# Weighed rows of the first sixteen expert blocks parked in DRAM until the edges are done

## The chip, the cores and the metric

The kernel runs on one core of one Trainium2 chip. Its time is the device time of one execution in microseconds (us). The profile is of one execution, with each instruction's start and duration on the engines: PE (TensorE; PEld is its weight loading), DVE (VectorE), ACT (ScalarE), POOL (GpSimd) and SP (SyncE, which here only issues DMAs).

## What is computed

A graph attention layer with a feed-forward net is followed by a mixture of experts. There are 6,250 nodes of 256 features, 100,000 edges sorted by their target, and 8 experts of which each token takes two. Cut to what matters:

```python
xn = layer_norm(x); h = (xn @ W).reshape(N, 8, 32)
e = leaky_relu(a_src[src] + a_dst[dst])
alpha = softmax of e over the edges of one dst
out = segment_sum(h[src] * alpha, dst) + xn @ W_res + bias
out = layer_norm(out)
x = x + out + gelu_tanh(out @ w1 + b1) @ w2 + b2

probs = softmax(norm(x) @ Wr + br);  top_p, top_idx = top_k(probs, 2)
y_e = gelu(ln_e(norm(x)) @ W1[e] + b1[e]) @ W2[e] + b2[e]      # W1[e]: 256 x 1024
x = x + sum over the two chosen e of weight_e * y_e
```

## The kernel before

**Stages.** First the node tables are written to DRAM (to about 115 us). Then the edges run, from the last target node down, in steps of four tiles of 128 edges: a step gathers the source rows (`fetch`, four indirect DMAs on POOL, L873), weighs them on DVE (`weigh`, L917 to L921) and adds them by target node on PE (`add_tiles`, L936). There are `NG` = 196 such steps, each spread over six steps of the program (`LASTST` = 6): the gather of a step is issued three steps ahead of its product on DVE, into four buffers, and the second to fourth gather of a step also wait for ACT's work of the step ahead. When the nodes of a unit (256 rows) have all their edges, the node net runs for them, their rows are stored to `out` and routed: each row goes, with its token's number and weights, into a list of rows for each expert in DRAM (`scatter`, indirect DMAs on POOL, L1470).

**Blocks.** As soon as an expert has 256 rows, a block of them can run, while edges are still going on. There are `NS` = 53 blocks, three of them half blocks. A block loads its expert's weights (1 MB each for the two products, L1525 and L1533) and its rows (L1541) by SP, runs the two products on PE (`up`, L1054, and `down`, L1067), adds the bias on DVE (`finish`, L1573, into `yb`, three buffers), multiplies by the token's weight on ACT (`weigh_block`, L856 through the helper `act`), and adds the result to the tokens' rows in `out` (`give_back`, L1583): for each 128 rows one indirect DMA on POOL that accumulates in DRAM. Since two blocks can hold the same token, the first accumulating DMA of a block waits until those of the block before have landed; the two of one block don't wait for each other.

**The planner.** The order of all work on each engine is fixed when the program is built. `task` names a piece of work with its engine, a cost and the tasks that must lie a number of steps before it; `run_tasks` goes through the list of waiting tasks at each step, oldest first, and issues what is due as long as its engine has room. The room of a step is 7.5 for PE and 2.6 for POOL while edges run (less what the edges take), and 3.9 and 2.6 behind them. A give-back costs 2.6, so a step takes one of them, or one scatter. SP's tasks cost nothing. Steps from `NG + LASTST` = 202 on have no edges; there the edges' buffers are given up and a third set of weight buffers is opened (L1662 to L1664). SP and POOL carry out their instructions in the program's order: one that waits holds up all behind it on that engine.

Of the kernel before, what the change touches and what calls it, by code (L numbers as in the profile page):

```python
# [45 lines left out]
F32 = mybir.dt.float32  # L46
# [9 lines left out]
P = 128  # L56
# [167 lines left out]
def gnn_moe_kernel(  # L224
# [28 lines left out]
    nc = tc.nc  # L253
    N, D = x.shape
# [36 lines left out]
    NG = len(order)  # L291
# [5 lines left out]
    BT = 256  # L297
    BJ = BT // P
    NB = (2 * N + E * (BT - 1)) // BT
    NS = min(NB, -(-(2 * N + E * BT // 2) // BT))  # L300
    NF = min(NS, -(-2 * N // BT) + 1)
    AHEAD = 3
    NX = NB + NS - NF + AHEAD

    turn_of = list(range(NF - (NS - NF)))
# [27 lines left out]
    dp = ctx.enter_context(tc.tile_pool(name="dram", bufs=1, space=DRAM))  # L333
    rp = ctx.enter_context(tc.tile_pool(name="route", bufs=1))
    gnn = ctx.enter_context(ExitStack())
# [13 lines left out]
    tab_m = dp.tile([NP + P, H], F32, name="tab_m")  # L349
    tab_e = dp.tile([NP + P, 2 * H], F32, name="tab_e")  # L350
    accd = dp.tile([NP + P, DA], F32, name="accd")


    acc_lo = gp.tile([P, KHI + 2, DA], F32, name="acc_lo")
# [157 lines left out]
    with ExitStack() as actx:  # L512
# [102 lines left out]
        for i0, (t0, t1) in enumerate(sets):  # L615
            n = t1 - t0
# [14 lines left out]
            for j in range(n):  # L631
                t = t0 + j
# [43 lines left out]
            for a, k0, b0, b1 in ((acc_lo, 0, t0, min(t1, KHI + 2)),  # L676
                                  (acc_hi, KHI, max(t0, KHI + 2), t1)):
                if b0 < b1:
                    m, i = b1 - b0, slice(b0 - t0, b1 - t0)
# [299 lines left out]
    LASTST = 6  # L979
# [16 lines left out]
    pending, urgent = [], []  # L996
    held = []

    def task(*a, **k):
        t = Task(*a, **k)  # L1000
        if urgent:
            pending.insert(urgent[0], t)
            urgent[0] += 1
        else:
            pending.append(t)
        return t
# [20 lines left out]
    def back(tasks, n):  # L1027

        return tasks[-n:][:1] if len(tasks) >= n else []
# [552 lines left out]
    def give_back(b, j, env):  # L1582
        st = nc.gpsimd.indirect_dma_start(  # L1583
            out=out, out_offset=bass.IndirectOffsetOnAxis(ap=tos[:, b, j:j + 1], axis=0),
            in_=env["yb"][:, j, :], in_offset=None, compute_op=ALU.add, bounds_check=N - 1,
            oob_is_err=False)
        tc.add_to_no_dep_group("given", st.ins)
        for i in env.setdefault("back", []):
            tc.declare_no_dep(st.ins, i, reason="a block holds a token once")
        env["back"].append(st.ins)  # L1590

    def block_loads(i):
        b = turn_of[i]
        env = {"n": 1 if NF <= b < NS else 2}
        env["units"], needs = next((u, d) for n, u, d in sure if n > b)
        free = [(d, 0) for d in blocks[i - 3:i - 2] + notes[i - 3:i - 2]] if i >= 3 else []

        env["pool"] = 1 if len(moew) > 1 and 1 not in pools[-2:] else 0
        user = [j for j in range(i) if pools[j] == env["pool"]][-2 + env["pool"]:][:1]
        if env["pool"] == 0 and pools.count(0) < 2:  # L1600
            user = []
        pools.append(env["pool"])
        env["lw"] = task(lambda: load_weights(b, env), "SP", 0.0,
                         [needs[-1], *[firsts_up[j] for j in user]])
        env["lw2"] = task(lambda: load_seconds(b, env), "SP", 0.0,
                          [env["lw"], *[blocks[j] for j in user]])
        env["lx"] = task(lambda: load_block(b, env), "SP", 0.0, [*needs, *free])
        env["lp"] = task(lambda: load_params(b, env), "DVE", 0.4, [needs[-1], *free])
        ahead.append((b, env))

    def block_unit(b, env):
        n = env["n"]
        no = task(lambda: note(b, env), "DVE", 0.6,
                  [(env["lx"], 2), *[(d, 0) for d in back(stored, 4)]])
        dn = net(env, lambda: env["xb"], [(env["lx"], 2), env["lp"]], lambda: env["w1"],
                 lambda: env["w"][1], AF.Gelu, lambda: env["pc"][:, 0, :],
                 more=[(env["lw"], 2)], scale=lambda: env["pc"][:, 0, KF:],
                 more2=[(env["lw2"], 2)])
        firsts_up.append(ups_[-1])
        fi = task(lambda: finish(env), "DVE", 0.35 * n, [dn, *[(d, 0) for d in back(stored, 3)]],  # L1620
                  free="py")
        wb_ = task(lambda: weigh_block(env), "ACT", 0.45 * n, [fi, no])
        for j in range(n):
            wb_ = task(lambda j=j: give_back(b, j, env), "POOL", 2.6, [wb_])
        stored.append(wb_)
        blocks.append(fi)
        notes.append(no)


    units = [(t, 2) for t in range(NT - 2, 0, -2)]  # L1630
    if NT % 2:
        units.append((0, 1))
    units = [(t, n, order.index((first_group(t), groups[first_group(t)][1] - 1)))
             for t, n in units]
# [5 lines left out]
    firsts_up = []  # L1640
    blocks, stored, cleared, sure, chunked, moew, last_hi, ahead = [], [], [], [], [0], [], [], []
    pools = []
    EARLY = 10
    final_list, there = [], None
    LATER = {6: (w1_sb, ffn_w1.rearrange("(k p) f -> p k f", p=P)),
# [4 lines left out]
    with tc.manual_schedule():  # L1650
        nc.sync.dma_start(xs[E * CAP:, :].rearrange("(p r) d -> p r d", r=2),
                          blank[:, None, :].to_broadcast([P, 2, DX]))
        while s < NG + LASTST or pending or u < len(units) or len(blocks) < NS:
            for g in range(s, min(s + EARLY, NG)):
                if chunk_of[order[g][0]] not in gds:
                    fetch_nodes(chunk_of[order[g][0]])
            for f, d in STAGES:
                if 0 <= s - d < NG:
                    f(s - d)
            if s in LATER:  # L1660
                nc.scalar.dma_start(*LATER[s])
            if s == NG + LASTST:  # L1662
                edges.close()
                moew.append(gnn.enter_context(tc.tile_pool(name="moew3", bufs=1)))  # L1664
            if len(firsts) < len(units) and len(firsts) <= s + 1:
                first_unit(len(firsts))
            if len(firsts) == len(units) and firsts[-1].step is not None and fp:
                first_.close()
                fp = None
            if last_hi and last_hi[0].step is not None and not moew and not fp:  # L1670
                hi_pool.close()
                moew.append(ctx.enter_context(tc.tile_pool(name="moew", bufs=2, side="right")))
            nb = len(blocks) + len(ahead)
            if moew and len(ahead) < 1 + len(moew) and nb < NS and any(n > turn_of[nb]
                                                                       for n, _, _ in sure):
                block_loads(nb)

            while sum(t.cost for t in pending if t.eng == "PE") < QUEUE:
                if (u < len(units) and units[u][2] <= s - LASTST
                        and not (ahead and was_nodes)):  # L1680
                    was_nodes = True

                    if u == len(units) - 1:
                        urgent.append(0)
                    if u not in loaded:
                        loaded[u] = node_loads(u)
                    node_unit(u, loaded[u])
                    since.append(u)
                    u += 1
                    if u < min(len(units), len(firsts)):  # L1690
                        loaded[u] = node_loads(u)
                    if u % 2 == 0 or u == len(units):
                        chunk_tasks(since, u == len(units), u == len(units) - 1)
                        since = []
                    urgent.clear()
                elif ahead:
                    was_nodes = False
                    block_unit(*ahead.pop(0))
                else:
                    break  # L1700
            room = dict(ROOM if s < NG + LASTST else ROOM_AFTER)
            if s < NG + LASTST:
                g = s - 5
                ends = 0 <= g < NG and order[g][1] == groups[order[g][0]][1] - 1
                for e in EDGES:
                    room[e] -= EDGES[e] + ends * BEHIND[e]
            run_tasks(s, room)
            acts.append([])
            s += 1
            if there is None and final_list and final_list[0].step is not None and len(blocks) > NS - 2:  # L1710
                there = nc.values_load(total[0:1, 0:1], min_val=0, max_val=NX)
        if NS < NX:
            with tc.If(there > NS):
                while pending or len(blocks) < NX:
                    nb = len(blocks) + len(ahead)
                    if len(ahead) < 2 and nb < NX:
                        block_loads(nb)
                    if ahead:
                        block_unit(*ahead.pop(0))
                    run_tasks(s, dict(ROOM_AFTER))  # L1720
                    s += 1
# [31 lines left out]
```

## Time and profile before

| | us |
|---|---|
| median of 3 runs (1726.76 to 1741.64) | 1732.98 |
| the profiled execution | 1733.02 |
| its span, first to last instruction | 1731.2 |
| PE busy, of the span | 1554.3 (90%) |
| POOL busy | 1154.3 (67%) |
| DVE busy | 982.9 (57%) |
| ACT busy | 803.4 (46%) |

```profile
PEclk9986899999988999999999999999999999999999
GB/s 208 265 207 220 153 189 154 157 173 165 140 141 213 210 185 208 169 245 166 208 221 201 176 236 197 223 188 204 197 210 218 220 203 207 260 112 238 191 220 41
L1470 POOL DMA_INDIRECT xs<-xe,slot x98 | 106.9, 1091 | 55.7 <-DMA w1b<-in_L_ffn_W_dram 21.4
L1573 DVE TENSOR_TENSOR yb<-py,b2b 128x512 f32<-128x512 f32 (+1 forms) x53 | 35.7, 673 | 153.5 <-PE py L1067 153.5
```

The first two lines give a value for each fortieth of the span (43.3 us): the granted clock of PE in tenths, and the rate of all DMAs. The others are groups of instructions: line, engine, operation, result and operands, number; then busy us and the mean ns of one; then the engine's idle time just before them and what ended most of it. In lines of a timeline the first two numbers are the start and the duration in us, and the bracket holds the idle time ahead. In the lines of stretches each engine's busy time is followed by its number of instructions, and the row ends with the clock, the busy share of the DMA engines and GB/s.

### The profile page before, as it was taken

To read this page: it belongs to the slowest core of one execution; us is meant where nothing else is said; L and a number is where in the kernel's file an instruction comes from. 1 tells how busy PE (TensorE), PEld (TensorE's weight loads), DVE (VectorE), ACT (ScalarE), POOL (GpSimd) and SP (SyncE) were. 2 spreads that over 40 slices of the span, in tenths; PEclk is the share of its full clock that TensorE was granted. 3 is DMA by queue.
4 is the path that set the end of the run, shared out by engine and by line. 5 is a ranking of instruction groups with operands and counts; after the bars stand their busy time and mean duration, and the time that the engine had idled before them with its cause. 6 is when DMAs were issued, how large, how long until landed. Compare 5 with 4: busy or idle time off the path is not lost.

```text
span 1731.2 us, 28987 instructions
## 1 busy us (share of the span) xinstructions
PE 1554.3 (90%) x8577; PEld 1252.8 (72%) x8577; DVE 982.9 (57%) x3512; ACT 803.4 (46%) x2063; POOL 1154.3 (67%) x1190
## 2 busy tenths in 40 slices
PE   4856898889877999999999999998988998899996
PEld 3644676667656878788888887786867887788885
DVE  6855788888888765766667564347334335131000
ACT  4843455554535554555555454444423433343332
POOL 4437777777777777777878778777777774412222
PEclk9986899999988999999999999999999999999999
DMA  6887565556546657586676676766677777847672
GB/s 208 265 207 220 153 189 154 157 173 165 140 141 213 210 185 208 169 245 166 208 221 201 176 236 197 223 188 204 197 210 218 220 203 207 260 112 238 191 220 41
DMA packets 232901, 334.93 MB, mean 193 GB/s; under 512 B 45169, under 2 KB 189082, under 8 KB 232734
## 3 DMA queue, kind: packets, MB, share of 16 engines
q1 hardware_dynamic: 170892, 190.31, 34.2%
q0 software_dynamic: 58944, 139.58, 30.9%
q10 hardware_dynamic: 2898, 3.09, 0.6%
q8 instruction: 71, 1.16, 0.3%
q14 instruction: 96, 0.79, 0.1%
HBM read 275.95 MB, written 61.10 MB: 195 GB/s over the span
## 4 chain that ended last, share of the span: by engine, by line
PE 51%; DMA 8%; DVE 7%; issue 4%; POOL 3%; ACT 2%; DVEq 0%; SPq 0%; POOLq 0%; ACTq 0%
PE ph L1054 21%; PE py L1067 21%; DMA gs<-tab_s,srce 6%; PE pl L936 3%; POOL gs L873 2%; DVE msg L921 2%; PE pt L1037 1%; PE pt L899 1%; PE pt L961 1%; ACT turned_in L856 1%; DMA out_dram<-yb,tos 1%; PE pz L907 1%; DMA w2b<-in_L_ffn_W_dram 1%; ACT ht L856 0%; PE ph L1209 0%
## 5 line engine op out<-in xcount | busy, mean ns | idle before, releaser
L873 POOL DMA_INDIRECT gs<-tab_s,srce x784 | 824.2, 1051 | 247.6 <-issue 163.6
L1054 PE MATMUL ph<-turned_in,w1b 128*128 128x256 f32 (+1 forms) x1696 | 420.6, 378 | 7.9 <-ACT turned_in L856 6.8
L1067 PE MATMUL py<-w2b,ht 128*128 128x256 f32 x1648 | 418.0, 383 | 5.4 <-DMA w2b<-in_L_ffn_W_dram 5.4
L1054 PEld LDWEIGHTS ph<-turned_in,w1b 128*128 128x128 f32 x1696 | 318.2, 193 | 54.5 <-ACT turned_in L856 10.4
L1067 PEld LDWEIGHTS py<-w2b,ht 128*128 128x128 f32 x1648 | 313.0, 193 | 47.2 <-issue 6.4
L856 ACT ACTIVATE ht<-ph,pc 128x256 f32<-128x256 f32 (+1 forms) x424 | 175.1, 465 | 365.3 <-PE ph L1054 365.0
L1583 POOL DMA_INDIRECT out_dram<-yb,tos x103 | 165.2, 1604 | 194.1 <-ACT yb L856 139.0
L921 DVE TENSOR_TENSOR msg<-gs,msg 128x1024 f32<-128x1024 f32 x196 | 240.4, 1226 | 7.0 <-DVE msg L920 0.4
L936 PE MATMUL pl<-msg,oh 128*32 128x264 f32 x1568 | 133.9, 414 | 81.1 <-DVE msg L921 80.9
L917 DVE TENSOR_TENSOR ww<-gs,fac 128x64 f32<-128x64 f32 x196 | 44.0, 224 | 281.8 <-DMA gs<-tab_s,srce 246.2
L1054 PE MATMUL ph<-turned_in,w_sb 128*128 128x256 f32 (+1 forms) x800 | 193.4, 382 | 6.0 <-ACT ht L856 5.0
L1067 PE MATMUL py<-w_sb,ht 128*128 128x256 f32 x784 | 190.2, 380 | 0.0
L1054 PEld LDWEIGHTS ph<-turned_in,w_sb 128*128 128x128 f32 x800 | 150.0, 194 | 27.5 <-ACT ht L856 6.3
L1067 PEld LDWEIGHTS py<-w_sb,ht 128*128 128x128 f32 x784 | 144.5, 190 | 25.0 <-issue 3.5
L1470 POOL DMA_INDIRECT xs<-xe,slot x98 | 106.9, 1091 | 55.7 <-DMA w1b<-in_L_ffn_W_dram 21.4
L856 ACT ACTIVATE ht<-ph,prm 128x256 f32<-128x256 f32 (+1 forms) x200 | 82.6, 467 | 121.3 <-PE ph L1054 121.1
L856 ACT ACTIVATE fac<-pz 128x64 f32<-128x64 f32 x196 | 44.0, 225 | 186.1 <-PE pz L907 117.3
L1573 DVE TENSOR_TENSOR yb<-py,b2b 128x512 f32<-128x512 f32 (+1 forms) x53 | 35.7, 673 | 153.5 <-PE py L1067 153.5
L856 ACT ACTIVATE added<-pt,here 128x264 f32<-128x264 f32 x220 | 93.8, 478 | 20.0 <-PE pt L961 13.0
L936 PEld LDWEIGHTS pl<-msg,oh 128*32 128x32 f32 x1568 | 32.0, 110 | 96.8 <-issue 52.7
L899 PEld LDWEIGHTS pt<-ident,oh 128*128 128x128 f32 x196 | 28.3, 144 | 96.4 <-issue 43.7
L973 DVE TENSOR_TENSOR acc_lo<-acc_lo,added 128x528 f32 x56 | 39.8, 710 | 88.8 <-ACT added L856 75.5
(358 smaller groups left out, 2041.2 us busy)
## 6 DMA issues: line engine op xcount, KB each, us to landing
w1b<-in_L_ffn_W_dram SPq DMA_DIRECT2D x53, 1024.0 KB
w2b<-in_L_ffn_W_dram SPq DMA_DIRECT2D x53, 1024.0 KB
xb<-xs SPq DMA_DIRECT2D x50, 260.0 KB
gs<-tab_s,srce POOLq DMA_INDIRECT x784
b2b<-in_L_ffn_b_dram SPq DMA_DIRECT2D x53, 128.0 KB
tab_s<-hg SPq DMA_DIRECT2D x12, 544.0 KB
xt_d<-xt SPq DMA_DIRECT2D x12, 512.0 KB
xtf<-xt_d SPq DMA_DIRECT2D x24, 256.0 KB
```

Of the source, the lines that this page charges most:

```text
L856: i = nc.scalar.activation(*a, **k)
L873: ld = nc.gpsimd.indirect_dma_start(out=gs[:, j, :], out_offset=None, in_=tab_s, in_offset=bass.IndirectOffsetOnAxis(ap=srce[:, t:t + 1], ...
L899: nc.tensor.transpose(po[:, 0, :P], live[s, "oh"].rearrange("p j r -> p (j r)"), ident)
L917: nc.vector.tensor_tensor(ww, gs[:, :, D:], live.pop((s, "pz")).rearrange("p (j c) -> p j c", j=G), op=ALU.mult)
L921: nc.vector.tensor_tensor(msg[:, :, :D].rearrange("p t (h d) -> p t h d", h=H), gs[:, :, :D].rearrange("p t (h d) -> p t h d", h=H), msg[: ...
L936: nc.tensor.matmul(pl[j * W32:(j + 1) * W32, :], oh[:, j, :], msg[:, j, :], start=i == 0, stop=last)
L973: nc.vector.tensor_add(to, to, live.pop((q, "p2")))
L1054: nc.tensor.matmul(ph[:, c % 2, :W], w1[:, k, c * P:(c + 1) * P], env["in"][:, k, :W], start=k == 0, stop=k == KD - 1)
L1067: nc.tensor.matmul(env["py"][:, j, :], env["ht", c][:, j * P:(j + 1) * P], w2[:, c, :], start=c == 0 and "row" not in env, stop=c == KF - 1)
L1470: st = nc.gpsimd.indirect_dma_start(out=xs, out_offset=bass.IndirectOffsetOnAxis(ap=slots[k][:n, t:t + 1], axis=0), in_=xes[u // 2][:n, pl ...
L1573: nc.vector.tensor_tensor(yb[:, :n], env["py"][:, :n], env["w"][2][:, None, :].to_broadcast([P, n, D]), op=ALU.add)
L1583: st = nc.gpsimd.indirect_dma_start(out=out, out_offset=bass.IndirectOffsetOnAxis(ap=tos[:, b, j:j + 1], axis=0), in_=env["yb"][:, j, :], ...
```

## The change

The first 16 blocks (`LATE`) give nothing back when they are done. SP stores their weighed rows to a DRAM tile `kept`, one step or more behind ACT's weighing. From step 202 on, one of them is taken up at every fourth step: SP reads its rows back into a tile of a new pool of three buffers, and two steps later or more POOL issues its two accumulating DMAs, now at a planner's cost of 1.3 each. `stored`, on which `note` and `finish` of later blocks depend, holds the store in place of the give-back for these blocks. The loop goes on until all 16 are taken up. The other 37 blocks are as before.

```diff
+    LATE = 16
...
+    kept = dp.tile([LATE * BT, D], F32, name="kept")
...
+    def keep(i, env):
+        n = env["n"]
+        nc.sync.dma_start(kept[i * BT:i * BT + n * P].rearrange("(j p) d -> p j d", p=P),
+                          env["yb"][:, :n])
+
+    def fetch_kept(i, env, pool):
+        n = env["n"]
+        yb = pool.tile([P, 2, D], F32, name="kept_yb")
+        nc.sync.dma_start(yb[:, :n],
+                          kept[i * BT:i * BT + n * P].rearrange("(j p) d -> p j d", p=P))
+        env["yb"] = yb
+
+    def late_unit(b, i, n, pool):
+        env = {"n": n}
+        t = task(lambda: fetch_kept(i, env, pool), "SP", 0.0, [(d, 0) for d in back(lates, 3)])
+        for j in range(n):
+            t = task(lambda j=j: give_back(b, j, env), "POOL", 1.3, [(t, 0 if j else 2)])
+        lates.append(t)
...
-        for j in range(n):
-            wb_ = task(lambda j=j: give_back(b, j, env), "POOL", 2.6, [wb_])
+        if len(blocks) < LATE:
+            i = len(blocks)
+            wb_ = task(lambda: keep(i, env), "SP", 0.0, [wb_])
+            late.append((b, i, n))
+        else:
+            for j in range(n):
+                wb_ = task(lambda j=j: give_back(b, j, env), "POOL", 2.6, [wb_])
         stored.append(wb_)
...
+    late, lates = [], []
...
-        while s < NG + LASTST or pending or u < len(units) or len(blocks) < NS:
+        while s < NG + LASTST or pending or u < len(units) or len(blocks) < NS or late:
...
                 moew.append(gnn.enter_context(tc.tile_pool(name="moew3", bufs=1)))
+                kp = gnn.enter_context(tc.tile_pool(name="kept", bufs=3))
+            if s >= NG + LASTST and (s - NG - LASTST) % 4 == 0 and late:
+                late_unit(*late.pop(0), kp)
```

## The prediction

> **What bounds the kernel now.** I read the page's slices first, then the busy times in four stretches, then the waits of two of them, then the timeline of GpSimd at the end. The slices:
>
> ```profile
> PE   4856898889877999999999999998988998899996
> POOL 4437777777777777777878778777777774412222
> DMA  6887565556546657586676676766677777847672
> ```
>
> PE is full but for the beginning, POOL stands at seven tenths as long as the edges run and falls at slice 34. Those seven tenths hide that POOL is full too:
>
> ```profile
> L873 POOL DMA_INDIRECT gs<-tab_s,srce x784 | 824.2, 1051 | 247.6 <-issue 163.6
> L1583 POOL DMA_INDIRECT out_dram<-yb,tos x103 | 165.2, 1604 | 194.1 <-ACT yb L856 139.0
> ```
>
> A gather is 1.05 us and 0.3 us of "issue" idle follows it almost every time, so four of a step cost 5.4 us; a give-back costs 1.60 + 0.3 = 1.9 us, two for a block. By stretch (columns: length, then busy us of PE, PEld, DVE, ACT, POOL):
>
> ```profile
> 150.00:600.00 450.00, 389.67 (x2239) 300.70 (x2238) 367.37 (x1308) 229.08 (x601) 345.81 (x366) 0.92 0.59 173
> 600.00:1050.00 450.00, 444.46 (x2566) 365.31 (x2565) 289.54 (x1019) 235.23 (x580) 354.73 (x351) 1.00 0.68 199
> 1050.00:1450.00 400.00, 370.07 (x2088) 300.77 (x2087) 178.82 (x572) 159.94 (x415) 315.81 (x290) 0.97 0.70 206
> 1450.00:1731.20 281.20, 253.12 (x1254) 218.54 (x1252) 45.45 (x199) 98.59 (x234) 67.96 (x57) 0.98 0.63 182
> ```
>
> From 600 to 1050 PE idles 5.5 of 450 us; from 1050 to 1450 it idles 29.9 of 400. POOL, with 0.3 us for each of its instructions, is full in both (354.7 + 351 x 0.27 = 450; 315.8 + 290 x 0.29 = 400). Who waits tells them apart (waits from 600 to 1050, then from 1050 to 1450: us, times, longest):
>
> ```profile
> DVE ww L917 <- DMA gs<-tab_s,srce: 24.2, 9, 6.2
> ...
> DVE ww L917 <- DMA gs<-tab_s,srce: 187.3, 39, 9.6
> ```
>
> In the first stretch VectorE seldom waits for a gather, in the second nearly always. Pairing each step's fourth gather with its product on VectorE (L917) by order gives the lead of POOL, end to start: on average 16.2 us in steps 56 to 77, 9.9 in 78 to 129, 3.8 from 130 on. POOL is a little slower than PE from 600, eats its lead until about 1040, and sets the pace from there to 1446.
>
> Whether PE is really full before 1050 needs care. The Trainium skill ("Perfetto Trace Analysis", Identifying the Most-Contended Engine) says matmul busy time misjudges PE and weight-load busy should be used; by that PE would have 19% to spare there (365 of 450) and the whole 61 us taken from POOL would show. Against it stand two pieces of the chain of waits, from this stretch and from the stage behind the edges, where no gather runs:
>
> ```profile
> 661.45 2.59 PE ph L1054 x12
> ...
> 1571.77 3.45 PE ph L1054 x16
> ```
>
> Both are 0.216 us an instruction, the pace of PE left alone. The stretch has 516 + 491 + 264 + 288 = 1559 such instructions (337 us) and 520 edge matmuls at 0.139 us (72 us), 409 us without transposes and small products. So I take it as bound by PE.
>
> **Part by part.** *Taken away:* the 32 give-backs of the first 16 blocks, which lie between 600 and 1076, 32 x 1.9 = 61 us of POOL. In that stretch PE sets the pace, so this doesn't shorten it by 61 us. POOL keeps its lead: 16.2 - 3.8 = 12.4 us more at step 141. From there it again needs 400/57 = 7.0 us a step against PE's 6.5 and eats the lead in some 25 of 54 steps, then sets the pace as before, 12.4 us earlier. Steps 136 to 141 already ran at POOL's pace; of PE's idle 4.2 us at 1050 to 1100 I add 1.6 for them (an estimate from their share). Gain 14 us. Bounds: 0 if something else paces the gathers (each waits for ScalarE's work of the step ahead), and 35 us, all of PE's idle time from 600 to 1450.
>
> *Added on SP, edge phase:* 16 stores of 256 KB, each waiting for ScalarE's weighing of one step ahead. Behind it in SP's order stand weight loads; they are issued 37 to 60 us before their first matmul from 600 to 1000, a step is 7 us, so nothing is late: 0, at most 1. The output buffer (three of them) is freed by this store, no later than by a give-back that trails by 8 to 40 us.
>
> *Added behind the edges:* 16 fetches of 256 KB on SP at planner steps 202, 206, ..., 262, each with two give-backs. At 1450 to 1500 the DMA share is 0.95 at 278 GB/s and PE waits 5.4 us for second weights; two fetches of 0.9 us there, ahead of them in the queue: 2 us (0 to 6; the SP row could also wait for edge buffers that its tile takes over).
>
> Next is the last scatter, for which SP's block load waits, and weight loads behind that:
>
> ```profile
> 1550.26 0.99 POOL L1470 DMA_INDIRECT xs<-xe,slot  x1 [10.82 <-DVE sf L1383]
> ...
> 1560.62 0.37 SPq L1541 DMA_DIRECT2D xb<-xs  x1
> ...
> 1568.58 0.60 PE L1037 MATMUL pt<-ident,xb 128*128 128x128 f32 x4
> ```
>
> POOL idles some 35 us from 1493 to 1550, and four late blocks go in, each 3.4 us of issue plus a landing. With landings as they are the scatter is 0 to 11 us late, and the block load has 5 us to spare: 2 us (0 to 8).
>
> *The end.* A block's first give-back waits until the one before has landed, since both add to the output:
>
> ```profile
> 1698.30 1.54 POOL L1583 DMA_INDIRECT out_dram<-yb,tos  x1 [16.13 <-ACT yb L856]
> 1700.15 1.54 POOL L1583 DMA_INDIRECT out_dram<-yb,tos  x1 [0.30 <-ACT ht L856]
> 1707.10 1.54 POOL L1583 DMA_INDIRECT out_dram<-yb,tos  x1 [5.40 <-ACT yb L856]
> 1715.97 1.54 POOL L1583 DMA_INDIRECT out_dram<-yb,tos  x1 [7.34 <-ACT yb L856]
> 1717.82 1.54 POOL L1583 DMA_INDIRECT out_dram<-yb,tos  x1 [0.30 <-issue]
> 1722.34 1.54 POOL L1583 DMA_INDIRECT out_dram<-yb,tos  x1 [2.98 <-DMA out_dram<-yb,tos]
> ```
>
> From 1717.82 to 1722.34 is 4.5 us from one group's last issue to the next group's first; a pair costs 1.85 + 4.5 = 6.4 us. Following the planner's loop with its costs, the kernel before has steps 0 to 262, PE's last product at 258 and the last give-back at 262 (the row at 1722.34). Late blocks 15 and 16 are fetched at 258 and 262. Number 15 may go at 260, but 260 to 262 belong to older tasks that use up POOL's room, so it goes at 263, and 16 at 264: two pairs behind the row that now ends the kernel, 2 x 6.4 = 12.8 us. The pairs before them fit where POOL now idles (16.1 before 1698, 7.3 before 1716). With a landing 0.7 us slower they don't all fit and the end is 16 us later, with 1.2 us slower 27 us: I take 13, with 6 (one pair behind) to 27 as ends.
>
> The Trainium skill ("DMA: Bandwidth & Descriptors", Anatomy of one DMA) gives about 2.0 us fixed, mostly the write's receipt, plus bytes; a pair would then come to an estimated 5.7 us and the two to 11.4. This trace has 2.98 us of wait behind the issue.
>
> Sum: -14 + 2 + 2 + 13 = +3 us, on the profiled execution's 1733.02 us (span 1731.2), which is the median of the runs shown, 1732.98: **1736 us**.
>
> **Rivals.** *POOL binds earlier than I think* (faster): all 35 us of PE idle time go and the end costs 13: 1733 - 35 + 13 = 1711. For it: POOL's rows are full from 600. Against: PE's own pace above.
>
> *The give-backs behind the edges become a chain* (slower): 16 + 19 groups follow each other on POOL, each waiting for a landing. At 6.4 us they take 224 of 285 us. Landings of 7 to 8 us exist (1671.99 to 1679.88); from an average of about 4.5 us instead of 3.8 the late pairs no longer fit between blocks. At 5.0: +27 at the end, and the late scatter at its bound, +8: 1733 - 14 + 2 + 8 + 27 = 1756, with less lead kept (8) 1762.
>
> *The lead is not kept* (no gain, the end still paid): 1733 + 17 = 1750.
>
> *It doesn't do what it says:* the steps are fixed when the program is built, so the 16 blocks do leave the edges; I give this nothing.
>
> **Numbers.** Forecast 0.60, POOL binds earlier 0.13, chain 0.17, lead lost 0.10. One per cent, about what can be told from no change, is 17 us: 1716 to 1750. Faster takes the first rival but for a little: 0.12; slower the chain and half of the lost lead: 0.22; within, 0.66. The forecast's own range is 1722 to 1750; to hold 8 in 10 it reaches to 1713 and 1757.
>
> **What would show it.** Right: the last gather near 1432 instead of 1444, the lead still near 16 us at step 130, PE idle from 1050 to 1450 near 18 us, two pairs of give-backs of fetched rows behind the last block's, 12 to 13 us between them and it. Wrong: VectorE waiting for gathers as much as before, PE idle behind the edges growing by more than 10 us, POOL waiting for landings all through that stage, or weight loads late in the edge phase because SP waits for ScalarE.

## The result and the profile after

The changed kernel takes 1754.67 us (median of 4 runs, 1754.46 to 1756.79), the kernel before 1732.39 in the same comparison: ratio 1.012, 95% interval 1.0091 to 1.0149. It is slower, by about 22 us instead of the 3 that the sum gave. It lies inside the wider range (1713 to 1757), near its upper end, and outside the forecast's own (1722 to 1750). The profiled execution took 1756.79 us, its span is 1755.0 (before 1731.2).

The slices of the changed kernel, to be laid beside those of before:

```profile
PE   5856898889878999999999999999889987999980
POOL 4437777777777686766768677778777762443334
...
DMA  6877564556456666675666667676677669677852
```

At the right edge PE falls to 8 and 0: in the last fortieth nothing multiplies any more, while POOL and the DMA engines go on. By stretch, in the columns of the prediction:

```profile
600.00:1050.00 450.00, 444.46 (x2567) 365.30 (x2566) 289.92 (x1014) 234.90 (x580) 316.36 (x332) 1.00 0.64 201
1050.00:1450.00 400.00, 379.50 (x2156) 308.81 (x2156) 187.11 (x603) 163.78 (x427) 311.29 (x282) 0.98 0.71 210
```

From 600 to 1050 POOL is busy for 38 us less and PE for the same 444.46 us, to the hundredth. From 1050 to 1450 PE's idle time falls from 29.9 to 20.5 us (the edges of the changed kernel end at 1435.9, so the last 14 us of this stretch are no longer edges). The edges did get shorter. What came back lies at the end; GpSimd's timeline there:

```profile
1717.89 1.54 POOL L1585 DMA_INDIRECT out_dram<-kept_yb,tos  x1 [2.48 <-DMA out_dram<-yb,tos]
1719.74 1.54 POOL L1585 DMA_INDIRECT out_dram<-kept_yb,tos  x1 [0.30 <-issue]
1724.21 1.54 POOL L1585 DMA_INDIRECT out_dram<-yb,tos  x1 [2.93 <-DMA out_dram<-kept_yb,tos]
1728.50 1.54 POOL L1585 DMA_INDIRECT out_dram<-yb,tos  x1 [2.75 <-DMA out_dram<-yb,tos]
1730.35 1.54 POOL L1585 DMA_INDIRECT out_dram<-yb,tos  x1 [0.30 <-issue]
1734.25 1.54 POOL L1585 DMA_INDIRECT out_dram<-yb,tos  x1 [2.36 <-DMA out_dram<-yb,tos]
1737.81 1.54 POOL L1585 DMA_INDIRECT out_dram<-kept_yb,tos  x1 [2.02 <-DMA out_dram<-yb,tos]
1739.66 1.54 POOL L1585 DMA_INDIRECT out_dram<-kept_yb,tos  x1 [0.31 <-issue]
1743.71 1.54 POOL L1585 DMA_INDIRECT out_dram<-kept_yb,tos  x1 [2.51 <-DMA out_dram<-kept_yb,tos]
1745.55 1.54 POOL L1585 DMA_INDIRECT out_dram<-kept_yb,tos  x1 [0.30 <-issue]
```

A group is what one block adds, two DMAs or, for a half block, one. In the kernel before, the last groups but the very last waited for ScalarE ("<-ACT yb"). Here every one waits for the group ahead of it to land. PE's last product ends at 1708.9; still to go are three groups of fetched rows, three of blocks that ScalarE had weighed by 1707.1, and the last block's own. Split at four points (give-backs by their start), the two spans compare so:

| us | before | after | difference |
|---|---|---|---|
| last gather ends | 1445.7 | 1435.9 | -9.8 |
| from there to PE's last product | 272.2 | 273.0 | +0.8 |
| from there to the last block's last give-back | 4.5 | 25.3 | +20.8 |
| from there to the last give-back of all | 0 | 11.3 | +11.3 |
| from there to the end | 8.9 | 9.4 | +0.5 |

The differences add up to 23.6; the spans differ by 23.8, which is rounding. Two lines of this table were in the prediction: the edges, and the two late pairs behind the last block. The third line, 20.8 us by which the last block itself comes late, was taken as nothing.

### The profile page after: what moved, and what is told of

Read it like the earlier page. It is cut to its first block, busy times and chain, and to the rows that moved or that the text cites. A ratio compares the mean times of both kernels' runs of the same rounds, so it can differ in the third digit from the quotient of the medians.

```text
span 1755.0 us, 29054 instructions
## 1 busy us (share of the span) xinstructions
PE 1551.1 (88%) x8577; PEld 1250.7 (71%) x8577; DVE 985.1 (56%) x3512; ACT 803.0 (46%) x2063; POOL 1154.6 (66%) x1190
## 5 line engine op out<-in xcount | busy, mean ns | idle before, releaser
L875 POOL DMA_INDIRECT gs<-tab_s,srce x784 | 824.2, 1051 | 296.1 <-issue 155.6
L1585 POOL DMA_INDIRECT out_dram<-yb,tos x71 | 114.5, 1613 | 108.9 <-ACT ht L858 58.7
L901 PEld LDWEIGHTS pt<-ident,oh 128*128 128x128 f32 x196 | 28.1, 143 | 98.6 <-issue 43.0
```

The lines of the kernel that those rows point to most:

```text
L875: ld = nc.gpsimd.indirect_dma_start(out=gs[:, j, :], out_offset=None, in_=tab_s, in_offset=bass.IndirectOffsetOnAxis(ap=srce[:, t:t + 1], ...
L901: nc.tensor.transpose(po[:, 0, :P], live[s, "oh"].rearrange("p j r -> p (j r)"), ident)
L1585: st = nc.gpsimd.indirect_dma_start(out=out, out_offset=bass.IndirectOffsetOnAxis(ap=tos[:, b, j:j + 1], axis=0), in_=env["yb"][:, j, :], ...
```

## The experiments

**Theory.** Behind the edges, POOL's give-backs have become one chain in which each group waits for the one ahead to land, and landings are long while weights are being loaded. From the first group of fetched rows at 1498.8 to the last at 1743.71 there are 33 groups, 7.65 us apart on average where I had put 6.4. Nearly all pairs move the same 256 KB. Two pieces of GpSimd's timeline of the changed kernel show the two kinds of landing:

```profile
1531.13 1.55 POOL L1585 DMA_INDIRECT out_dram<-kept_yb,tos  x1 [6.55 <-issue]
1532.98 1.55 POOL L1585 DMA_INDIRECT out_dram<-kept_yb,tos  x1 [0.30 <-issue]
1537.56 1.55 POOL L1585 DMA_INDIRECT out_dram<-yb,tos  x1 [3.03 <-ACT ht L858]
1539.41 1.55 POOL L1585 DMA_INDIRECT out_dram<-yb,tos  x1 [0.30 <-issue]
1543.94 1.55 POOL L1585 DMA_INDIRECT out_dram<-kept_yb,tos  x1 [2.97 <-issue]
...
1561.16 1.54 POOL L1585 DMA_INDIRECT out_dram<-yb,tos  x1 [7.31 <-ACT turned_in L858]
1563.00 1.54 POOL L1585 DMA_INDIRECT out_dram<-yb,tos  x1 [0.30 <-issue]
1571.23 1.54 POOL L1585 DMA_INDIRECT out_dram<-kept_yb,tos  x1 [6.68 <-DMA kept_yb<-kept]
1573.07 1.54 POOL L1585 DMA_INDIRECT out_dram<-kept_yb,tos  x1 [0.30 <-issue]
1582.73 1.56 POOL L1585 DMA_INDIRECT out_dram<-yb,tos  x1 [8.11 <-ACT ht L858]
```

The bracket of a group's first row is its wait behind the group ahead. In the upper piece the groups of 1531.13 and 1537.56 have no loads beside them, and the groups behind them wait 3.03 and 2.97 us (the 6.55 of the first row belongs to the group ahead of it, which had loads beside it). In the lower piece there are loads beside every group, and the waits are 6.7 to 8.1 us. The releaser named is often ScalarE, or none at all ("issue"); that the landing is what is waited for is read from the records of the DMA packets below, by which the next group goes out 0.6 to 1.3 us behind the last packet of the one ahead, in all 32 cases but one. The same in the rows of stretches, one group each (after the engines' columns: clock, busy share of the DMA engines, GB/s):

```profile
1531.10:1537.60 6.50, 6.50 (x32) 5.72 (x31) 0.83 (x7) 2.03 (x5) 3.14 (x3) 1.00 0.36 40
1589.00:1598.80 9.80, 9.80 (x49) 8.64 (x48) 1.32 (x5) 3.84 (x9) 3.09 (x2) 1.00 0.97 295
1717.90:1724.20 6.30, 0.00 (x0) 0.00 (x0) 0.23 (x1) 0.51 (x1) 3.08 (x2) 0.50 0.38 44
```

With the DMA engines at 0.36 a pair takes 6.4 us, at 0.97 it takes 9.8. The third row is at the program's end, the place from which I had taken the 6.4 in the kernel before: nothing is loaded there. The records of the DMA packets say where in the landing the time lies. Pairs with under 0.5 MB of SP's loads beside them, which are mostly weights (14): first packet 2.17 us after the issue, last 5.22, next group's issue at 6.24. Pairs with 1.2 MB and more (13): 3.79, 8.90 and 10.14. The packets begin later and take 5.1 instead of 3.1 us. But a longer wait also lets more loads pass, so this division alone doesn't say which is the cause; the fifth experiment does.

**Rivals.** The cost is POOL's issue time and the fetches themselves; or it is the rhythm of every fourth step; or it comes from the edges, whose end the change moved against the blocks; or a chain of such groups has long landings whatever runs beside it.

Four kernels ran on one chip, on which the kernel before takes 1939.52 us (13 runs), four on another with 1934.25 (23 runs), four on a third with 1742.94 (17 runs). Ratios are to the kernel before on the same chip; differences in us are taken inside one chip only. The split is that of the table above, of one profiled execution each. The times that e1 to e4 were expected to take were worked out for a chip with 1732 us. On the two slower chips the edges gained more than there (without the late additions, e1, the kernel is 30 and 21 us faster than before, where the edges of the first profile gave 10), so that whole times and ratios tell the expectations apart poorly; the split does.

| run | chip | median | ratio (95%) | last block behind PE | late groups behind it | end behind PE |
|---|---|---|---|---|---|---|
| changed, again | third | 1757.74 | 1.010 (1.007 to 1.013) | 25.1 | 11.6 | 46.2 |
| e1, again | first, second | 1909.19, 1913.31 | 0.983 (0.976 to 0.991), 0.989 (0.981 to 0.997) | 4.6, 4.4 | 0 | 13.5, 13.2 |
| e2 | first | 1972.42 | 1.0125 (1.004 to 1.021) | 20.9 | 11.3 | 45.0 |
| e3 | first | 1948.59 | 1.004 (1.001 to 1.008) | 14.6 | 0 | 23.8 |
| e4, again | first, second | 1922.65, 1918.38 | 0.988 (0.982 to 0.995), 0.993 (0.990 to 0.997) | 4.2, 4.4 | 9.6, 9.6 | 23.2, 23.5 |
| e8 | second | 1925.69 | 0.994 (0.991 to 0.997) | 10.9 | 11.2 | 31.5 |
| e5 | third | 1738.95 | 0.9986 (0.997 to 1.0003) | 4.6 | 0 | 13.7 |
| e6 | third | 1713.93 | 0.984 (0.982 to 0.987) | 4.3 | 0 | 13.6 |
| e7 | third | 1712.32 | 0.9835 (0.981 to 0.986) | 4.4 | 0 | 13.6 |
| e9 | second | 1915.68 | 0.991 (0.987 to 0.995) | 10.8 | 0 | 19.8 |

**The late additions left out (e1).**

```diff
-                late_unit(*late.pop(0), kp)
+                late.pop(0)
```

> The change with its second half left out: the first 16 blocks' rows are stored to DRAM, but never read back and never added to the output. Theory A (the loss lies wholly behind the edges, where 16 late groups and 19 others follow each other on POOL and each waits for the landing of the one before): the edge phase keeps its gain of about 10 us, PE's last product ends near 1709 us as in the changed kernel, and the end behind it is again the 13 us of the kernel before: span near 1722 us, ratio to before 0.994. Rival B (the stores on SP, which wait for ScalarE, or the traffic cost something in the edges or behind them): span of 1731 us or more.

The end lies 13.5 us behind PE, as in the kernel before, and 300.4 us behind the last gather. So the whole cost is in reading the rows back and adding them late, and the edges alone give a gain: ratio 0.983. That is more than the 0.994 expected. The edge phase of this chip is slower for every kernel run on it, and no trace of the kernel before was taken there, so the size of its gain on this chip stays open. The run was repeated on the second chip:

> The late additions left out once more (the first 16 blocks are missing in the output), beside the three others of this call. Theory: edges as in the changed kernel, the end 13 to 14 us behind PE, ratio 0.990 to 0.996 where the edge phase goes at the pace of the first runs. Rival (the edges themselves were made no shorter): ratio 0.998 or more.

13.2 us and 0.989, with an interval that holds the expected values. The rival falls: without the late additions the kernel is faster.

**The give-backs in the edges kept, and the late ones too (e2).** The first 16 blocks are added twice; the edges get back POOL's 32 instructions.

```diff
-            wb_ = task(lambda: keep(i, env), "SP", 0.0, [wb_])
+            task(lambda: keep(i, env), "SP", 0.0, [wb_])
             late.append((b, i, n))
-        else:
-            for j in range(n):
-                wb_ = task(lambda j=j: give_back(b, j, env), "POOL", 2.6, [wb_])
+        for j in range(n):
+            wb_ = task(lambda j=j: give_back(b, j, env), "POOL", 2.6, [wb_])
```

> The late half without the relief: the first 16 blocks are given back in the edge phase as before, and are also stored, fetched and added once more behind the edges (their rows count twice). Theory A: the edges end where they did before, near 1446 us, and the chain of 35 groups behind them costs what it does in the changed kernel, some 33 us between PE's last product and the end more than before: 1762 to 1768 us. Rival C (only the two pairs behind the last block count, at 6.4 us each, as the prediction had it): 1746 to 1750 us.

From the last gather to the end it takes 332.7 us, 32.3 more than e1 on the same chip; in the changed kernel it was 33.6 more than before. The cost of the end is the same whether the edges are relieved or not: the rival of the edges falls. The ratio alone, 1.0125, wouldn't show it: Theory A's times are ratios of 1.017 to 1.021, rival C's 1.008 to 1.010, and the interval holds both. The last gather is 37 us later than in e1 (1647.8 against 1610.2), the price of the edge phase with its give-backs and the stores together; by the medians, 63.2 us apart, it is nearer 31, for e2's profiled execution was its slowest.

**Every third step instead of every fourth (e3).**

```diff
-            if s >= NG + LASTST and (s - NG - LASTST) % 4 == 0 and late:
+            if s >= NG + LASTST and (s - NG - LASTST) % 3 == 0 and late:
```

> The changed kernel with a late block at every third step instead of every fourth, so that the last is fetched at step 247 instead of 262 and none stands behind the last block on POOL. Theory A: the number of groups, and so of landings that are waited for one after another, is the same, and so is the backlog: 1748 to 1758 us. Rival C (the late pairs behind the last block are the cost): they are gone, so 12 us or more come off: 1735 to 1742 us.

No group of fetched rows is left behind the last block, and the end lies 23.8 us behind PE, so it looks as if the rhythm were at fault; the ratio, 1.004, too is that of rival C (1.002 to 1.006), not of Theory A (1.009 to 1.015). But from the last gather to the end it takes 332.4 us, 32.0 more than e1: nothing was saved, and the ratio is low because of the edges' larger gain on this chip: by the medians e3 takes 39 us more than e1. PE's last product now comes 308.6 us behind the last gather instead of 287.0. The backlog stands ahead of the blocks instead of behind them, and PE waits for it through the output buffers. The waits of e3 behind the edges show the way (engine, operation, line, for what: us in all, times, longest):

```profile
DVE yb L1575 <- DMA out_dram<-yb,tos: 44.7, 4, 17.9
POOL out_dram L1585 <- DMA out_dram<-kept_yb,tos: 31.1, 6, 7.2
ACT yb L858 <- DVE yb L1575: 27.3, 4, 12.7
```

VectorE can't write the next product into one of the three output buffers until a give-back has landed, in waits of up to 17.9 us.

**The late additions into another tensor (e4).** The same rows are fetched and as many DMAs are issued, but they add to a DRAM tensor that nobody else writes then, so the two kinds don't wait for each other's landings.

```diff
-    def give_back(b, j, env):
+    def give_back(b, j, env, to=None):
...
-            out=out, out_offset=bass.IndirectOffsetOnAxis(ap=tos[:, b, j:j + 1], axis=0),
+            out=out if to is None else to, out_offset=bass.IndirectOffsetOnAxis(ap=tos[:, b, j:j + 1], axis=0),
...
-            t = task(lambda j=j: give_back(b, j, env), "POOL", 1.3, [(t, 0 if j else 2)])
+            t = task(lambda j=j: give_back(b, j, env, res_d), "POOL", 1.3, [(t, 0 if j else 2)])
```

> The changed kernel, but its late additions go to another DRAM tensor of the same shape that nothing reads any more, so that they and the blocks' additions to the output no longer wait for each other's landing; bytes, instructions and order are the same, the output lacks the first 16 blocks. Theory A (the waits for landings are the cost): most of the 33 us goes; PE ends near 1709 us and the last pairs end some 20 to 24 us behind it: 1729 to 1735 us. Rival D (the accumulating transfers themselves, or POOL's issue, are too slow beside the weight loads): 1750 us or more.

The last block comes 4.2 us behind PE, as in the kernel before. From the last gather to the end it takes 309.5 us, 9.1 more than e1, against 32.3 with the waits. So 23 of the 32 us are waits of the two kinds for each other's landings, and the rest is what e4 still has, two pairs behind the last block. The ratio, 0.988, is below the 0.998 to 1.002 of Theory A's times, again with the larger gain of the edges. GpSimd's timeline of this run shows fetched rows going out right behind a block's:

```profile
1705.40 1.54 POOL L1585 DMA_INDIRECT out_dram<-yb,tos  x1 [6.03 <-ACT yb L858]
1707.25 1.55 POOL L1585 DMA_INDIRECT out_dram<-yb,tos  x1 [0.30 <-issue]
1709.11 1.55 POOL L1585 DMA_INDIRECT res_d<-kept_yb,tos  x1 [0.30 <-issue]
1710.96 1.55 POOL L1585 DMA_INDIRECT res_d<-kept_yb,tos  x1 [0.30 <-issue]
```

> The late additions go to another DRAM tensor once more (the first 16 blocks are missing in the output), so that they and the 37 other groups no longer wait for each other's landings. Theory (two thirds or more of the 33 us are waits for landings): the end 20 to 26 us behind PE, ratio 0.995 to 1.002, some 8 to 12 us above the kernel without late additions. Rival (what costs is the fetches and POOL's issue time): ratio 1.008 or more.

On the second chip it is 10.0 us more than e1 (306.0 against 296.0), with the end 23.5 us behind PE; the ratio, 0.993, is a little under the expected 0.995. (By the medians e4 takes 13.5 us more than e1 on the first chip and 5.1 on the second; the split is the steadier measure.) The rival, that the fetches and the issue time are what costs, falls.

**Half of the weight traffic behind the edges (e8).** Blocks whose weights are loaded from step 202 on load half of each matrix and use it twice; the products are as many.

```diff
+        env["half"] = s >= NG + LASTST
+        kn = KD // 2 if env["half"] else KD
-        nc.sync.dma_start(w1b, W1[bass.ds(e, 1)].rearrange("e (k p) f -> p (e k) f", p=P))
+        nc.sync.dma_start(w1b[:, :kn],
+                          W1[bass.ds(e, 1), :kn * P].rearrange("e (k p) f -> p (e k) f", p=P))
...
-            nc.tensor.matmul(ph[:, c % 2, :W], w1[:, k, c * P:(c + 1) * P], env["in"][:, k, :W],
+            nc.tensor.matmul(ph[:, c % 2, :W], w1[:, 0 if env.get("half") else k, c * P:(c + 1) * P],
+                             env["in"][:, k, :W],
```

(and the same for the second matrix)

> The changed kernel, but blocks whose weights are loaded from step 202 on load only the first half of each weight matrix and use it twice: the same products, half of the weight traffic behind the edges, another output. Theory (weight loads under way lengthen the landings that POOL's groups wait for): fewer groups lie behind landings of 6 to 9 us, the mean wait behind a group falls from about 4.7 us to about 3.8 or less, the end lies 15 to 25 us behind PE's last product instead of 46, ratio to the kernel before 0.993 to 1.003. Rival (a chain of groups has long landings whatever else is moved): the end stays 40 us or more behind PE, ratio about 1.01.

The end lies 31.5 us behind PE, between the two expectations and outside both. Of the 32.7 us by which the end had grown, halving the traffic took 14.6, near half of it; I had expected 21 or more. The ratio, 0.994, is in the theory's interval. During the 32 waits from the first fetched group on, SP's loads (weights, and the rows of blocks and of late groups, the latter alike in both kernels) moved 16.4 MB instead of 28.1, the mean wait fell from 4.43 to 3.97 us, and the first 32 groups lie 7.24 us apart instead of 7.71. Over 31 distances that is 14.5 us, as much as the end came nearer. So the traffic does lengthen landings: the rival of a chain that is slow whatever runs beside it falls. My size for it was too large: 9 pairs still had 1.2 MB and more beside them and took 9.4 us. What the other half of the traffic costs wasn't tried. This comparison crosses two chips; e2, on a chip as slow, has 45.0 us behind PE where the changed kernel has 46.1 and 46.2, so the chip is hardly what changed the end.

**Fewer blocks, and which ones (e5, e6, e7, e9).** If the chain is what costs, fewer late groups leave it gaps. And if PE sets the pace until about 1040, it matters which blocks are taken out of the edges. The changed kernel ran beside them.

> The changed kernel as it is, beside the others of this set. Theory A: behind the last gather 319 us pass to the end as in its first profile (286 in the kernel before), and the last product of PE is some 46 us before the end (13 before).

The first eight blocks (e5):

```diff
-    LATE = 16
+    LATE = 8
```

> The changed kernel with 8 late blocks, the first 8, instead of 16; the last is fetched at step 230. Theory A: 27 groups instead of 35 at some 8 us each fit behind the edges beside the blocks, so the end behind PE's last product is again 13 to 16 us; the edges keep only part of the lead (POOL takes up its old pace from step 107 on) and gain 4 to 8 us: ratio to before 0.995 to 1.000. Rival E (what is late costs its own landing, block by block, wherever it stands): half of the loss stays, ratio 1.004 to 1.01.

Blocks 16 to 23 (e6):

```diff
-    LATE = 16
+    LATE, LATE0 = 8, 16
...
-        if len(blocks) < LATE:
-            i = len(blocks)
+        if 0 <= len(blocks) - LATE0 < LATE:
+            i = len(blocks) - LATE0
```

> Eight late blocks again, but those of which the give-backs fall where POOL sets the pace: numbers 16 to 23 instead of 0 to 7 (steps 142 to 168). Theory A with the lead of POOL as the edges' measure: 30 us come off POOL where it is the bound, PE has some 14 us to spare there and a lead of 12 us is rebuilt: edges 18 to 28 us shorter, end as before: ratio 0.984 to 0.991. Rival F (it doesn't matter which blocks): as with the first eight, 0.995 to 1.000.

Blocks 16, 18 and so on to 30 (e7):

```diff
-    LATE = 16
+    LATE, LATE0 = 8, 16
...
-        if len(blocks) < LATE:
-            i = len(blocks)
+        if (len(blocks) - LATE0) % 2 == 0 and 0 <= len(blocks) - LATE0 < 2 * LATE:
+            i = (len(blocks) - LATE0) // 2
```

> Eight late blocks spread over the whole stretch where POOL sets the pace: numbers 16, 18, ..., 30. Theory A: the same 30 us come off POOL, and PE's idle time of 30 us there can be used from end to end without a lead that runs full: edges 22 to 30 us shorter, ratio 0.982 to 0.988, a little under that of blocks 16 to 23. Rival F: 0.995 to 1.000.

The changed kernel repeats itself: 1.010, the end 46.2 us behind PE. With eight late blocks, whichever of the three sets, the end is back at 13.6 to 13.7, so rival E falls. GpSimd's timeline of e7 at the end looks like that of before, the groups but the last waiting for ScalarE:

```profile
1688.71 1.54 POOL L1585 DMA_INDIRECT out_dram<-yb,tos  x1 [5.40 <-ACT yb L858]
1697.59 1.54 POOL L1585 DMA_INDIRECT out_dram<-yb,tos  x1 [7.34 <-ACT yb L858]
...
1703.91 1.54 POOL L1585 DMA_INDIRECT out_dram<-yb,tos  x1 [2.93 <-DMA out_dram<-yb,tos]
```

The three differ in the edges, though each takes 16 give-backs (30 us of POOL) out of them. From step 60 to step 195 the product on VectorE gains 1 us against the kernel before in e5 (4 to 8 were expected: a miss), 27 in e6 (18 to 28 expected), 23 in e7 (22 to 30). It does matter which blocks, so rival F falls. In e5, POOL's lead is 17.9 us at step 78 and 2.0 at step 126: what the first eight blocks gave was used up by the later ones before POOL began to set the pace. VectorE's waits for gathers from 1050 to 1450 say the same (us in all, times, longest). Of e5:

```profile
DVE ww L919 <- DMA gs<-tab_s,srce: 186.9, 39, 10.6
```

Of e6:

```profile
DVE ww L919 <- DMA gs<-tab_s,srce: 83.3, 21, 10.0
```

Of e7:

```profile
DVE ww L919 <- DMA gs<-tab_s,srce: 139.3, 31, 9.8
```

e5 waits as much as the kernel before (187.3 us). e6 and e7 beat both kernels, by 1.6% against the one before; between the two the intervals overlap, so the order that was expected of them isn't shown.

Twelve, every second one from 12 to 34 (e9, e7's edit with `LATE, LATE0 = 12, 12`):

> Twelve late blocks, every second one from 12 to 34. Theory (the late groups cost nothing until POOL's chain behind the edges is gapless; 8 leave it gaps, 16 do not): the last gather comes 3 to 5 us earlier than with the eight of e7, the end lies 13 to 20 us behind PE, ratio 0.980 to 0.988. Rival (each late group beyond eight costs about 4 us at the end, 33 us over eight blocks): end 28 to 32 us behind PE, ratio 0.990 to 0.995.

With twelve late blocks the end lies 19.8 us behind PE, the last block 10.8, so the chain begins to cost something between 8 and 12 late blocks (on another chip, and with other blocks than those of e5 to e7). The theory's 13 to 20 us hold, at their edge; the ratio, 0.991, is above what was expected of it. The rival's ratio fits, its 28 to 32 us behind PE don't. e7 didn't run on that chip, so whether twelve is better or worse than eight stays open.

## Why the prediction came out as it did

*The edges* (-14): right in mechanism, near in size. The last gather is 9.8 us earlier, and this execution began its steps 1.8 to 2.0 us later, so about 12; in the repeat it was 13.6 us earlier. The lead was kept as described: 15.3 us on average in steps 78 to 129 where it had been 9.8, 12.3 at step 132 where it had been 2.0, and after step 144 POOL set the pace again. It was used up sooner than the prediction had it, which let it last some 25 steps from step 141. VectorE's waits for gathers from 1050 to 1450 fell from 187.3 us to 142.4:

```profile
DVE ww L919 <- DMA gs<-tab_s,srce: 142.4, 33, 9.8
```

Where the prediction was loose: it counted on the lead of all 16 blocks, and e5 shows that the first eight alone give next to nothing (1 us).

*PE sets the pace from 600 to 1050*: right. PE is busy for 444.46 us of it in both kernels, though POOL lost 38 us of work. The Trainium skill's rule ("Perfetto Trace Analysis", Identifying the Most-Contended Engine) would have given PE room there by its weight-load busy time, 365.30 of 450 us (of the two measures that the section names; the other, MFU, wasn't worked out here). In the changed kernel and in e5, with 25 and 16 give-backs fewer by then, the product on VectorE gained nothing from step 60 to step 126 (0.0 us in both), which speaks against it here.

*The stores on SP* (0): right; no weights came late in the edges.

*Two fetches and the late scatter* (+2 and +2): together +0.8, from the last gather to PE's last product. The scatter came 2.6 us earlier than before (1547.67) and thus some 7 us late against the edges, within the bounds of 0 to 11, and the cover of 5 us held most of it. (GpSimd's idle time from 1493 to 1550, put at some 35 us, is 43 in the trace of before, 12.3 of them waits for landings.)

*The end* (+13): the step that failed, by its size. Its two parts went apart. "Two pairs behind the row that now ends the kernel", 12.8 us, measured 11.3. "The pairs before them fit where POOL now idles" did not hold: the last block came 20.8 us late. The term rested on a landing of 3.8 us, taken from the last rows of the trace of before, where SP loads nothing. Over the 32 waits of the chain the mean behind a group was 4.43 us where that row has 2.98, so the landing in the prediction's terms was 3.8 + 1.45, about 5.2. The chain was also a little longer than counted, 37 groups behind the last gather instead of 35. The prediction had put the limit from which the chain forms at about 4.5, and the chain's price at a landing of 5.0 at 1756; the kernel took 1754.67. So the rival held, at a chance of 0.17, and with it one of the signs of being wrong: POOL waits for landings through all of that stage. That the range held is luck as far as the forecast goes, for its own range ended at 1750; the wider one had been drawn out to cover part of this rival. That the rival's 1756 is so near is in part luck too: it had 14 us off the edges where 9.8 came, 10 for the fetches and the scatter where 0.8 came, and 27 at the end where 32.6 came.

The evidence for the rival stood in the trace of before: landings of 7 to 8 us between 1671.99 and 1679.88, which were noted as existing and not averaged, and right behind the edges three groups in a row whose wait of 5 to 7 us the trace itself puts down to the landing:

```profile
1490.29 1.55 POOL L1583 DMA_INDIRECT out_dram<-yb,tos  x1 [5.62 <-DMA out_dram<-yb,tos]
1500.95 1.54 POOL L1583 DMA_INDIRECT out_dram<-yb,tos  x1 [7.25 <-DMA out_dram<-yb,tos]
1509.40 1.54 POOL L1583 DMA_INDIRECT out_dram<-yb,tos  x1 [5.04 <-DMA out_dram<-yb,tos]
```

The Trainium skill has a rule that fits the two kinds of landing in part ("DMA: Bandwidth & Descriptors", Queues, rings and completion order): each DMA engine serves the queue rows that have work in turn, a packet at a time. An estimate from it doubles the 3.1 us of a pair's packets beside a weight load, to 6.2; the records have 5.1. Why the first packet also comes 1.6 us later stays open; no run here shows it.

Summed anew: -9.8 + 0.8 + 20.8 + 11.3 + 0.5 = +23.6 on 1733.02, 1756.6 us; the profiled execution took 1756.79.

## What to carry to other kernels

A latency is read in the stage where it will be paid: the same accumulating DMA let the next one go 6.2 us after a pair's issue where hardly anything was loaded and 10.1 beside weight loads, and a chain of 33 of them made the last block 21 us late. When work is moved into the gaps of a later stage, add up the whole stage with the loaded price, groups times price against its length, before looking for gaps that seem to fit. And move only what binds where it stands: the give-backs of the first eight blocks had cost the edges next to nothing (1 us), while eight from the stretch that POOL sets (e6, e7) gave 23 to 27 us there and left the chain its gaps.

## What the runs showed of the hardware

The wait of an accumulating DMA for the one ahead of it, both into the same tensor, ran in the changed kernel from 2.0 us (behind a single tile, nothing else moving) over 2.9 to 3.1 (a pair) to 9.5 with 2.0 MB of SP's loads moved meanwhile.

Two of the chips took 1934 and 1940 us for the kernel before, 11 to 12% more than the 1733 and 1743 of the others, with a mean granted clock of 0.912 to 0.928 in their traces against 0.954 to 0.965. A gather took less there (1027 ns on average in e1's repeat against 1051 in the changed kernel), so POOL's gathers aren't what is slower. Their traces hold waits, mostly of ScalarE, that are put down to "remote", to no instruction of this core; the traces of the other chips have none. Of e1's repeat, the largest two:

```profile
ACT fac L858 <- remote: 60.1, 12, 13.2
ACT ht L858 <- remote: 59.5, 12, 13.9
```

All such waits that it lists come to about 249 us. Whether they are the cause wasn't tried, and they overlap with other waits; the end behind PE was the same on all chips (13.2 to 13.7 us without a chain, 45.0 to 46.2 with it).
